# Two heads of four turned in 32x32 squares by VectorE, gathered step by step, with four small moves between engines

## The chip, the cores and the metric

The kernel runs on one core of a Trainium2 chip. The metric is device microseconds of one execution, lower is better; the median of several executions is given. All data are float32. The engines are TensorE (PE in the profile, PEld its weight loads), VectorE (DVE), ScalarE (ACT), GpSimd (POOL) and SyncE (SP), which here only issues DMAs.

## The reference

Two layers run on 8 samples of 512 tokens by 512 features.

The first is a graph attention: features of the tokens and of a condition go through a linear layer; each token attends with 16 heads, in two directions, to the first 20 tokens of its sample; the result goes through a relu and is added to the input. The change doesn't touch it.

The second is a self-attention between two conditioned layer norms:

```python
h = sln(hidden, w)                       # gamma(w) * layernorm(hidden) + beta(w)
q, k, v = split(h @ Wqkv.T + bqkv)       # 16 heads of 32
energy = einsum('bhqd,bhkd->bhqk', q, k)
att = softmax(energy, axis=-1) / D ** 0.5
out = einsum('bhqk,bhkd->bhqd', att, v)
h1 = (out @ Wp.T + bp) + hidden
return sln(h1, w) + h1
```

## The kernel before

The first layer takes the start of the program, to about 397 us of the span. The rest is the second layer, in 128 steps: a step is one batch (sample) b, one group g of four heads and one block c of 128 query tokens, 16 steps to a batch. `at` is the number of the step in its batch. The 112 steps of the first seven batches run in one loop, written out by hand (no scheduler reorders it: each engine runs its instructions in the order of the code); the last batch's 16 steps run in a loop of their own. All of the following is one iteration, step n.

*Scores.* `scores(n + 1)` makes the energies of four heads on TensorE, four heads at a time in four groups of 32 rows, into two pairs of PSUM banks (tile s). `tops` takes the negated maxima of each row on VectorE (one instruction for head 0, one for head 1, one for heads 2 and 3). `exps` takes the exponentials on ScalarE into tiles e, with the sum of each row. Only two pairs of s exist, so the next scores of a pair wait for its exponentials.

*Turning.* For the product with v the exponentials must lie with the keys in the partitions. `turn_probs` does this for a head with four transposes on TensorE into a bank (tile pt), and `keep_probs` copies the bank to turned_et on ScalarE. Heads 0, 1 and 2 go this way (`BY_BLOCK = 3`): heads 0 and 1 at the end of the step before, head 2 behind the scores. Head 3 goes through `turn_blocks`: VectorE transposes its 32x32 squares in place of one another (tile blocks), two steps into one tile; `put_out` writes that tile to DRAM (squares) in every odd step, and in the even step after it `gather` reads it back with four DMAs, one for each block of 32 partitions, so that the squares come to lie where a whole transpose would have put them (tile gathered). Both go through SP's queue, with the loads of tokens (`fetch`), the gates (`load_gate`) and the stores of results.

*Product with v.* In odd steps `weigh_two` multiplies both steps' turned exponentials by v, the four heads side by side in four groups of 32 columns of pao; heads 0 to 2 are of the steps just done, head 3 is two steps older. Every four steps `outputs` copies pao to ao on ScalarE and `divide` applies the sums on GpSimd.

*Projections.* Each step has two slots for products of other batches, listed in `JOBS`: the q, k and v products of the next batch and the output projection of the one before. They are made by a scheme of seven products of halves instead of eight (`product`, `output_product`): each fills a bank and VectorE adds it to where it belongs; the first of the seven (n = 1) is only copied, or gets its bias. The scheme's sums of operands are on GpSimd. These products, the turned heads, the turned tokens (`turn`, tile pz) and the sums' factors (`spread`, tile pr) share three PSUM banks in rotation (`bank`), so a product waits until the bank three allocations earlier has been emptied.

*Norms.* `statistics` (VectorE, with one power on GpSimd) and `norm` make the first norm's z for the batch after next in steps 13 to 15; `finish` does the second norm of the batch before in steps 7 to 12: statistics and norm on VectorE, then three sums on GpSimd and a store. In the code a step's statistics stand behind its two products and the exchange of squares.

Of the kernel before, what the change touches and what calls it, by code (L numbers as in the profile page):

```python
# [19 lines left out]
P = 128  # L20
# [24 lines left out]
def graph_then_self_attention(ctx: ExitStack, tc: tile.TileContext, x, x_t, near, near_t, labels, w_self_t, wq, wk_t,  # L45
# [679 lines left out]
    bp = ctx.enter_context(tc.tile_pool(name="bp", bufs=2, reuse_waits="tile"))  # L725
# [57 lines left out]

    def product(b, i, n):

        a = {1: lambda: a_(i, 0, 0), 2: lambda: a_(i, 0, 1), 3: lambda: SUMS[i, 3], 4: lambda: a_(i, 1, 1),
             5: lambda: SUMS[i, 0], 6: lambda: SUMS[i, 1], 7: lambda: SUMS[i, 2]}[n]()
        t = {1: lambda: quarter(HT[b], 0, 0), 2: lambda: quarter(HT[b], 1, 0), 3: lambda: quarter(HT[b], 1, 1), 4: lambda: SUMS["t", 3],
             5: lambda: SUMS["t", 0], 6: lambda: SUMS["t", 1], 7: lambda: SUMS["t", 2]}[n]()
        out = bank(f"pst_{b}_{i}_{n}").rearrange("p (m n) -> p m n", m=2)  # L790
        fixed, moving = (t, a) if i == 2 else (a, t)
        for m in range(2):
            for k in range(2):
                nc.tensor.matmul(out[:, m, :], fixed[:, k, m * P:(m + 1) * P], moving[:, k, :], start=(k == 0), stop=(k == 1))  # L794
# [12 lines left out]
        if n == 1 and i < 2:  # L807
            bias_2 = col["b_q" if i == 0 else "b_k"][:, 2:4].unsqueeze(2).to_broadcast([P, 2, M])
            nc.vector.tensor_tensor(c_(1, 0), out, bias_2, ALU.add)
        elif n == 1:  # L810
            nc.vector.tensor_copy(c_(1, 0), out)
        for dst, src in {2: [((0, 0), (1, 0))], 6: [((1, 0), (1, 0))], 5: [((1, 1), (1, 0))], 3: [((0, 1), (1, 1))],
                         4: [((1, 0), (1, 0))], 7: [((1, 1), (1, 1)), ((1, 0), (1, 0))]}.get(n, ()):
            if i < 2 and n in (2, 3):
                for j in range(2):
                    nc.vector.scalar_tensor_tensor(c_(*dst)[:, j, :], out[:, j, :], b_less[:, i, j:j + 1], c_(*src)[:, j, :], ALU.add, ALU.add)
            else:
                nc.vector.tensor_tensor(c_(*dst), out, c_(*src), ALU.add)
# [9 lines left out]
    def output_product(b, n):  # L828
# [135 lines left out]
    def spread(m):  # L964
# [7 lines left out]
    BY_BLOCK = 3  # L972
    turned_et = tp.tile([P, 2, BY_BLOCK, C, P], F32, name="turned_et")
    gathered = xp.tile([P, C, F], F32, tag="x", name="gathered").rearrange(
        "p k f -> p (k f)").rearrange(
        "p (i r k c q) -> p i r k c q", i=2, r=4, k=C, c=2)
# [12 lines left out]
    def keep_probs(n, j, copy):  # L989
        pt = PT[n, j]  # L990
        if j < BY_BLOCK:
            et = turned_et[:, n % 2, j]
        else:
            et = bp.tile([P, C, P], F32, tag="blocks", name=f"et_{n}_{j}")
# [3 lines left out]
    def turn_blocks(n):  # L998

        if n % 2 == 0:  # L1000
            BLOCKS[n // 2] = bp.tile([P, 4, C, 2, DH], F32, tag="blocks", name=f"blocks_{n // 2}")
        nc.vector.transpose(BLOCKS[n // 2][:, :, :, n % 2, :].rearrange("p s k q -> p k s q"),  # L1002
                            E[n][BY_BLOCK].rearrange("p (k s q) -> p k s q", k=C, s=4))

    def put_out(m):

        OUT[m] = dram.tile([P, 4, C * 2 * DH], F32, tag="squares", bufs=3, name=f"squares_{m}")
        nc.sync.dma_start(OUT[m], BLOCKS[m].rearrange("p s k c q -> p s (k c q)"))

    def gather(m):  # L1010

        by_chunk = OUT[m].rearrange("(r p) s e -> s p r e", r=4)
        for s in range(4):
            nc.sync.dma_start(gathered[DH * s:DH * (s + 1), m % 2].rearrange("p r k c q -> p r (k c q)"), by_chunk[s])
# [14 lines left out]
    def weigh_two(m):  # L1029

        for k in range(C):
            for j in range(4):
# [5 lines left out]
                moving = turned_et[:, :, j, k, :] if j < BY_BLOCK else gathered[:, m % 2 ^ 1, :, k].rearrange("p r c q -> p c r q")  # L1038
# [46 lines left out]
    from_v3 = made(v, 3) + made(q, 1, 2) + made(v, 7, 4) + made(q, 6, 5)  # L1085
    JOBS = {0: own + made(v, 1, 2, 6, 5) + from_v3 + made(k, 1, 2, 6) + [None] + made(q, 3) + end}
# [5 lines left out]
    JOBS[B - 2][14:] = (made(v, 3) + made(q, 1, 2) + [None] + made(q, 6, 5) + made(k, 1) + [None] + made(k, 2, 6) + made(q, 3)  # L1092
# [25 lines left out]
    def job(b, slot):  # L1118
# [11 lines left out]
        elif kind == "late":  # L1130
            product(b, *of)
        elif kind == "output":
# [4 lines left out]
    with tc.manual_schedule():  # L1137
# [16 lines left out]
        for j in range(BY_BLOCK - 1):  # L1154
            turn_probs(0, j)

        for n, (b, g, c) in enumerate(steps[:ALONE]):
            at = n % 16
            scores(n + 1)
            turn_probs(n, BY_BLOCK - 1)  # L1160
            for j in range(BY_BLOCK - 1):
# [5 lines left out]
            keep_probs(n, BY_BLOCK - 1, nc.scalar.copy)  # L1167
            if n > 4 and n % C == 2:
                divide(n // C - 1)
            turn_blocks(n)  # L1170
            if n % C == C - 1:
# [10 lines left out]
            if n == 5:  # L1182
                values_bias()
# [9 lines left out]
            if n % 2:  # L1193
                weigh_two(n // 2)
            if n % 2 == 0 and n > 0:
                gather(n // 2 - 1)
            elif n % 2:
                put_out(n // 2)
            if b == 0:
                weight_sums((v, q, k, 3)[at // 4], at % 4)  # L1200
            finish_parts(b, "statistics")
            if b + 2 < B:
                for i in {13: (0, 1), 14: (2, 3)}.get(at, ()):
                    norm_stats(b + 2, i)
# [3 lines left out]
            finish_parts(b, "sums")  # L1208
            if at != 4:
                add_gathered()  # L1210
            exps(n + 1, range(4))
            if n + 1 < ALONE:
                for j in range(BY_BLOCK - 1):
# [18 lines left out]
        for n in range(ALONE, len(steps)):  # L1232
# [27 lines left out]
            if at == 0:  # L1260
                spread(n // C - 1)
                outputs(n - 1, slice(0, DH * BY_BLOCK))
                gather(n // 2 - 1)
# [80 lines left out]
```

## Time and profile before

| what | value |
|---|---|
| runs | 1316.15, 1312.71, 1314.56 us; median 1314.56 |
| profiled execution | 1310.33 us; its span 1308.5 us |
| granted TensorE clock | 0.999 |
| TensorE busy | 1283.5 us, 98% of the span |
| VectorE, ScalarE, GpSimd busy | 960.2 (73%), 740.6 (57%), 627.9 us (48%) |
| a steady batch (16 steps) | 111.78 us; TensorE 111.30, VectorE 82.70, ScalarE 78.72, GpSimd 50.77 busy |
| DMA queue of SP | 142.30 MB, 32.8% of 16 engines' time |

A row of the profile names the line of the kernel, the engine, the operation, the tiles written and read, and the number of instructions; then busy time, mean duration in ns, and idle time of the engine just before them with what ended it. The chain that ended last follows the program back from its last instruction, at each piece to what released it. SPq is SyncE issuing DMAs.

### The profile page before, as it was taken

The numbers are of one execution on the slowest core, as the hardware profiler recorded it, in microseconds if no ns is written. First come the engines' busy times: TensorE is split into PE (matmuls) and PEld (weight loads), VectorE is DVE, ScalarE is ACT, GpSimd is POOL, SyncE is SP. The second block draws the span as 40 slices with busy tenths as digits, with TensorE's granted clock in tenths as the row PEclk, the third lists the DMA queues.
The fourth block names the chain that finished last, engine by engine and source line by source line (L and its number), as shares of the span: only waits on it lengthen the run. The fifth ranks groups of instructions, "written<-read, shape, count | busy, mean of one in ns | idle before, by whom it ended". The sixth has DMA issues, their size and how long they took to land.

```text
span 1308.5 us, 24813 instructions
## 1 busy us (share of the span) xinstructions
PE 1283.5 (98%) x9227; PEld 917.2 (70%) x9227; DVE 960.2 (73%) x1675; ACT 740.6 (57%) x1790; POOL 627.9 (48%) x537
## 2 busy tenths in 40 slices
PE   9999999999999999999999999999999999999997
PEld 6567887777764577677777767667776776766775
DVE  4479897888745568768858766876876777676887
ACT  2333233323224666767776676676667677676664
POOL 0067765677650112337235623733643363373776
PEclk9999999999999999999999999999999999999999
DMA  9533552253221132413422342432243243233010
GB/s 343 181 110 104 191 195 104 84 178 111 92 76 46 65 98 65 146 65 121 134 85 81 130 129 65 151 124 82 90 133 118 72 139 133 78 111 101 9 42 34
DMA packets 90486, 144.42 MB, mean 110 GB/s; under 512 B 14272, under 2 KB 47488, under 8 KB 90368
## 3 DMA queue, kind: packets, MB, share of 16 engines
q1 hardware_dynamic: 89936, 142.30, 32.8%
q8 instruction: 74, 1.21, 0.4%
q10 hardware_dynamic: 432, 0.55, 0.1%
q14 instruction: 44, 0.36, 0.1%
HBM read 95.97 MB, written 46.85 MB: 109 GB/s over the span
## 4 chain that ended last, share of the span: by engine, by line
PE 90%; DVE 7%; ACT 1%; POOL 1%; issue 1%; DMA 0%; POOLq 0%; DVEq 0%; ACTq 0%
PE pst L794 19%; PE pt L987 15%; PE s L929 12%; PE pao L1039 8%; PE pss L533 8%; PE psp L837 6%; PE psf_p L360 4%; PE psf L313 2%; PE pqk L139 2%; PE po L577 2%; PE ppj L865 2%; PE pw L502 1%; PE ptw L565 1%; PE pq L483 1%; PE pao L1026 1%; PE pv L139 1%
## 5 line engine op out<-in xcount | busy, mean ns | idle before, releaser
L934 DVE TENSOR_REDUCE top<-s 128x1 f32<-128x512 f32 (+1 forms) x369 | 306.5, 884 | 96.3 <-PE s L929 96.1
L948 ACT ACTIVATE e<-s,top 128x512 f32<-128x512 f32 x512 | 345.6, 692 | 44.8 <-DVE top L934 43.5
L996 ACT COPY turned_et<-pt 128x512 f32<-128x512 f32 x369 | 205.8, 592 | 200.3 <-PE pt L987 200.2
L987 PEld LDWEIGHTS pt<-ident,e 128*128 128x128 f32 x1600 | 174.8, 140 | 132.1 <-issue 60.0
L987 PE MATMUL pt<-ident,e 128*128 128x128 f32 x1600 | 230.7, 280 | 4.6 <-ACT e L948 3.2
L929 PE MATMUL s<-k_pair,q_pair 32*128 32x512 f32 x992 | 159.4, 640 | 0.0
L533 PE MATMUL pss<-kq,sf 128*128 128x320 f32 x512 | 142.9, 432 | 0.0
L1064 POOL TENSOR_TENSOR ao_pair<-ao_pair,factor 128x512 f32<-128x512 f32 x28 | 36.8, 1313 | 188.3 <-ACT ao_pair L1059 188.3
L533 PEld LDWEIGHTS pss<-kq,sf 128*128 128x128 f32 x512 | 94.9, 190 | 36.1 <-ACT kq L490 0.3
L1039 PE MATMUL pao<-turned_et,v 128*32 128x256 f32 x1344 | 107.9, 382 | 0.0
L948 ACT ACTIVATION_READ_ACCUMULATOR e<-s,top 128x1 f32 x512 | 107.3, 209 | 0.0
L1039 PE MATMUL pao<-gathered,v 128*32 128x256 f32 x448 | 107.2, 382 | 0.0
L1002 DVE STREAM_TRANSPOSE blocks<-e 128x512 f32<-128x512 f32 x112 | 79.0, 706 | 23.2 <-ACT e L948 22.9
L1039 PEld LDWEIGHTS pao<-turned_et,v 128*32 128x32 f32 x1344 | 49.9, 109 | 48.3 <-issue 13.5
L539 POOL TENSOR_TENSOR t<-t,mask 128x640 f32<-128x640 f32 x32 | 49.5, 1546 | 65.3 <-DVE t L537 65.3
L554 ACT ACTIVATE t<-t 128x640 f32<-128x640 f32 x32 | 23.6, 738 | 93.3 <-POOL t L551 93.3
L929 PEld LDWEIGHTS s<-k_pair,q_pair 32*128 32x128 f32 x992 | 48.1, 182 | 29.6 <-issue 18.5
L559 POOL TENSOR_TENSOR t<-t,den 128x640 f32<-128x640 f32 x32 | 40.7, 1272 | 56.3 <-DVE den L558 55.7
L551 POOL TENSOR_TENSOR t<-t,top 128x640 f32<-128x640 f32 x32 | 47.3, 1480 | 39.0 <-DVE top L550 39.0
L961 POOL TENSOR_SCALAR wide<-dens 128x512 f32<-128x512 f32 x28 | 42.1, 1503 | 48.8 <-ACT turned_et L996 34.7
L97 POOL TENSOR_TENSOR mv<-mv,minus_half 128x1 f32<-128x1 f32 x32 | 19.6, 611 | 92.7 <-DVE mv L96 92.7
L956 POOL TENSOR_SCALAR e<-e,den 128x512 f32<-128x512 f32 x63 | 46.3, 735 | 28.0 <-DVE den L953 18.7
(290 smaller groups left out, 2572.8 us busy)
## 6 DMA issues: line engine op xcount, KB each, us to landing
squares<-blocks SPq DMA_DIRECT2D x56, 512.0 KB
gathered<-squares SPq DMA_DIRECT2D x224, 128.0 KB
x<-in_x SPq DMA_DIRECT2D x8, 1024.0 KB
mid<-x SPq DMA_DIRECT2D x32, 256.0 KB
xq<-mid SPq DMA_DIRECT2D x8, 1024.0 KB
out<-o SPq DMA_DIRECT2D x31, 256.0 KB
vt<-in_x_t SPq DMA_DIRECT2D x7, 1024.0 KB
xn<-mid SPq DMA_DIRECT2D x7, 1024.0 KB
```

Source lines behind the costliest of these rows:

```text
L360: nc.tensor.matmul(o[:, m, :], a[:, k, m * P:(m + 1) * P], t[:, k, :], start=(k == 0), stop=(k == 1))
L533: nc.tensor.matmul(o, SF[b][:, k, cut], KQ[b][:, k, on], start=(k == 0), stop=(k == C - 1))
L539: nc.gpsimd.tensor_tensor(t, t, MASK[b][:, c, None].to_broadcast([P, H, D2]), ALU.mult)
L794: nc.tensor.matmul(out[:, m, :], fixed[:, k, m * P:(m + 1) * P], moving[:, k, :], start=(k == 0), stop=(k == 1))
L837: nc.tensor.matmul(out[:, m, :], t[:, k, m * P:(m + 1) * P], a[:, k, :], start=(k == 0), stop=(k == 1))
L929: nc.tensor.matmul(S[n][j // 2][:, j % 2, :], Q[b, g][on, c * P:(c + 1) * P], K[b, g][on, :], start=True, stop=True)
L934: nc.vector.tensor_reduce(top, S[n][pair][:, j:j + len(heads)], AX.X, ALU.max, negate=True)
L948: nc.scalar.activation(e, S[n][j // 2][:, j % 2, :], AF.Exp, bias=TOP[n, j], accum_out=den)
L987: nc.tensor.transpose(pt[:, k * P:(k + 1) * P], E[n][j][:, k * P:(k + 1) * P], ident)
L996: copy(et, pt.rearrange("p (k n) -> p k n", k=C))
L1002: nc.vector.transpose(BLOCKS[n // 2][:, :, :, n % 2, :].rearrange("p s k q -> p k s q"), E[n][BY_BLOCK].rearrange("p (k s q) -> p k s q", ...
L1039: nc.tensor.matmul(pao[DH * j:DH * (j + 1), c * P:(c + 2) * P], V[b][:, k, DH * h:DH * (h + 1)], moving, start=(k == 0), stop=(k == C - 1))
```

## The change

- `BY_BLOCK` is 2: head 2 joins head 3 on VectorE's way, so `turn_blocks` has two transposes per step, into one tile per step. `put_out` and `gather` run in every step, right behind `turn_blocks`; a step's squares are gathered in the next one. The pool of blocks has one buffer instead of two, and there are two tiles gathered instead of two halves of one.
- The transposes of both remaining heads stand at the end of the step before, ahead of `weigh_two` in odd steps; none stands behind the scores.
- The first of each seven products is emptied by ScalarE instead of VectorE. These copies are kept in `LATER` and run between the exponentials of heads 1 and 2.
- z is made by GpSimd instead of VectorE, from batch 2 on.
- A step's statistics move ahead of its products, right behind the maxima.
- In `JOBS` some products change places, v's and q's within a step above all; the product for the values' bias becomes a job.

```diff
-        nc.vector.tensor_scalar(Z[b][:, c, :], (src or XN[b])[:, c, :], mv[:, 0:1], mv[:, 1:2], ALU.subtract, ALU.mult)
+        engine = nc.gpsimd if src is None and b > 1 else nc.vector
+        engine.tensor_scalar(Z[b][:, c, :], (src or XN[b])[:, c, :], mv[:, 0:1], mv[:, 1:2], ALU.subtract, ALU.mult)
...
-    bp = ctx.enter_context(tc.tile_pool(name="bp", bufs=2, reuse_waits="tile"))
+    bp = ctx.enter_context(tc.tile_pool(name="bp", bufs=1, reuse_waits="tile"))
...
-            bias_2 = col["b_q" if i == 0 else "b_k"][:, 2:4].unsqueeze(2).to_broadcast([P, 2, M])
-            nc.vector.tensor_tensor(c_(1, 0), out, bias_2, ALU.add)
+            for j in range(2):
+                LATER.append(lambda j=j, dst=c_(1, 0): nc.scalar.activation(
+                    dst[:, j, :], out[:, j, :], AF.Identity, bias=col["b_q" if i == 0 else "b_k"][:, 2 + j:3 + j]))
         elif n == 1:
-            nc.vector.tensor_copy(c_(1, 0), out)
+            LATER.append(lambda dst=c_(1, 0): nc.scalar.copy(dst, out))
...
-                nc.vector.tensor_copy(Y[b], out)
+                LATER.append(lambda dst=Y[b]: nc.scalar.copy(dst, out))
...
-    BY_BLOCK = 3
+    BY_BLOCK = 2
...
     def turn_blocks(n):
-        if n % 2 == 0:
-            BLOCKS[n // 2] = bp.tile([P, 4, C, 2, DH], F32, tag="blocks", name=f"blocks_{n // 2}")
-        nc.vector.transpose(BLOCKS[n // 2][:, :, :, n % 2, :].rearrange("p s k q -> p k s q"),
-                            E[n][BY_BLOCK].rearrange("p (k s q) -> p k s q", k=C, s=4))
+        BLOCKS[n] = bp.tile([P, 4, C, 2, DH], F32, tag="blocks", name=f"blocks_{n}")
+        for h in range(2):
+            nc.vector.transpose(BLOCKS[n][:, :, :, h, :].rearrange("p s k q -> p k s q"),
+                                E[n][BY_BLOCK + h].rearrange("p (k s q) -> p k s q", k=C, s=4))
...
-    from_v3 = made(v, 3) + made(q, 1, 2) + made(v, 7, 4) + made(q, 6, 5)
...
-                   + from_v3 + made(k, 1, 2, 6) + made(q, 3) + [None] + end)
+                   + made(q, 1) + made(v, 3) + made(q, 2) + made(v, 7, 4) + made(q, 6) + made(k, 1) + made(q, 5)
+                   + made(k, 2, 6) + [None] + made(q, 3) + end)
...
             scores(n + 1)
-            turn_probs(n, BY_BLOCK - 1)
-            for j in range(BY_BLOCK - 1):
+            for j in range(BY_BLOCK):
                 keep_probs(n, j, nc.scalar.copy)
...
             turn_blocks(n)
+            put_out(n)
+            if n > 0:
+                gather(n - 1)
...
+            finish_parts(b, "statistics")
+            if b + 2 < B:
+                for i in {13: (0, 1), 14: (2, 3)}.get(at, ()):
+                    norm_stats(b + 2, i)
             if 0 < at <= C:
                 turn(b + 1, at - 1)
...
             job(b, 2 * at)
             finish_parts(b, "norm")
             job(b, 2 * at + 1)
-            if n % 2:
-                weigh_two(n // 2)
-            if n % 2 == 0 and n > 0:
-                gather(n // 2 - 1)
-            elif n % 2:
-                put_out(n // 2)
...
-            finish_parts(b, "statistics")
...
+            exps(n + 1, (0, 1))
+            for after in LATER:
+                after()
+            LATER.clear()
             if at != 4:
                 add_gathered()
-            exps(n + 1, range(4))
+            exps(n + 1, (2, 3))
             if n + 1 < ALONE:
-                for j in range(BY_BLOCK - 1):
+                for j in range(BY_BLOCK):
                     turn_probs(n + 1, j)
...
+            if n % 2:
+                weigh_two(n // 2)
```

More of the change, by code (lines that the diff above doesn't have):

```diff
@@ L782, in graph_then_self_attention @@
     b_less = w1.tile([P, 2, 2], F32, name="b_less")
+    LATER = []
     def product(b, i, n):
@@ L970, in spread @@
         nc.scalar.copy(factor, pr)
-    BY_BLOCK = 3
+    BY_BLOCK = 2
     turned_et = tp.tile([P, 2, BY_BLOCK, C, P], F32, name="turned_et")
-    gathered = xp.tile([P, C, F], F32, tag="x", name="gathered").rearrange(
-        "p k f -> p (k f)").rearrange(
-        "p (i r k c q) -> p i r k c q", i=2, r=4, k=C, c=2)
+    gathered = [xp.tile([P, C, F], F32, tag="x", name="gathered_0").rearrange("p k f -> p (k f)"),
+                tp.tile([P, C * F], F32, name="gathered_1")]
+    gathered = [t.rearrange("p (c r k h q) -> p c r k h q", c=2, r=4, k=C, h=2) for t in gathered]
     pao = ps_a.tile([P, 512], F32, tag="pao", name="pao")
@@ L993, in keep_probs @@
         else:
-            et = bp.tile([P, C, P], F32, tag="blocks", name=f"et_{n}_{j}")
+            et = gathered[0][:, n % 2].rearrange("p r k h q -> p (r k h q)").rearrange("p (j k n) -> p j k n", j=2, k=C)[:, j - BY_BLOCK]
         ET[n, j] = et
@@ L998, in turn_blocks, with put_out, gather @@
     def turn_blocks(n):
-        if n % 2 == 0:
-            BLOCKS[n // 2] = bp.tile([P, 4, C, 2, DH], F32, tag="blocks", name=f"blocks_{n // 2}")
-        nc.vector.transpose(BLOCKS[n // 2][:, :, :, n % 2, :].rearrange("p s k q -> p k s q"),
-                            E[n][BY_BLOCK].rearrange("p (k s q) -> p k s q", k=C, s=4))
[L1005 to L1012, printed above, removed]
+        BLOCKS[n] = bp.tile([P, 4, C, 2, DH], F32, tag="blocks", name=f"blocks_{n}")
+        for h in range(2):
+            nc.vector.transpose(BLOCKS[n][:, :, :, h, :].rearrange("p s k q -> p k s q"),
+                                E[n][BY_BLOCK + h].rearrange("p (k s q) -> p k s q", k=C, s=4))
+    def put_out(n):
+        OUT[n] = dram.tile([P, 4, C * 2 * DH], F32, tag="squares", bufs=3, name=f"squares_{n}")
+        nc.sync.dma_start(OUT[n], BLOCKS[n].rearrange("p s k h q -> p s (k h q)"))
+    def gather(n):
+        by_chunk = OUT[n].rearrange("(r p) s e -> s p r e", r=4)
         for s in range(4):
-            nc.sync.dma_start(gathered[DH * s:DH * (s + 1), m % 2].rearrange("p r k c q -> p r (k c q)"), by_chunk[s])
+            nc.sync.dma_start(gathered[n // 2 % 2][DH * s:DH * (s + 1), n % 2].rearrange("p r k h q -> p r (k h q)"), by_chunk[s])
     def weigh(n):
@@ L1037, in weigh_two @@
                 h = 4 * g + j
-                moving = turned_et[:, :, j, k, :] if j < BY_BLOCK else gathered[:, m % 2 ^ 1, :, k].rearrange("p r c q -> p c r q")
+                moving = turned_et[:, :, j, k, :] if j < BY_BLOCK else gathered[m % 2 ^ 1][:, :, :, k, j - BY_BLOCK, :]
                 nc.tensor.matmul(pao[DH * j:DH * (j + 1), c * P:(c + 2) * P], V[b][:, k, DH * h:DH * (h + 1)],
@@ L1084, in graph_then_self_attention @@
     end = made(k, 5, 3) + first + fifth + made(q, 4, 7)
-    from_v3 = made(v, 3) + made(q, 1, 2) + made(v, 7, 4) + made(q, 6, 5)
-    JOBS = {0: own + made(v, 1, 2, 6, 5) + from_v3 + made(k, 1, 2, 6) + [None] + made(q, 3) + end}
+    JOBS = {0: own + made(v, 1) + [("values_bias",)] + made(v, 2, 6) + made(q, 1) + made(v, 5, 3) + made(q, 2) + made(v, 7, 4)
+            + made(k, 1) + made(q, 6, 5) + made(k, 2, 6) + made(q, 3) + end}
     for b in range(1, B - 1):
@@ L1089, in graph_then_self_attention @@
                    + made(v, 2, 6) + [("output", 1, 7)] + made(v, 5) + [("output", 1, 4)]
-                   + from_v3 + made(k, 1, 2, 6) + made(q, 3) + [None] + end)
-    JOBS[B - 2][14:] = (made(v, 3) + made(q, 1, 2) + [None] + made(q, 6, 5) + made(k, 1) + [None] + made(k, 2, 6) + made(q, 3)
+                   + made(q, 1) + made(v, 3) + made(q, 2) + made(v, 7, 4) + made(q, 6) + made(k, 1) + made(q, 5)
+                   + made(k, 2, 6) + [None] + made(q, 3) + end)
+    JOBS[B - 2][14:] = (made(q, 1) + made(v, 3) + made(q, 2) + [None] + made(q, 6, 5) + made(k, 1) + [None] + made(k, 2, 6) + made(q, 3)
                         + made(k, 5, 3) + made(q, 4) + [None] + made(q, 7) + made(k, 4) + made(k, 7))
@@ L1131, in job @@
             product(b, *of)
+        elif kind == "values_bias":
+            values_bias()
         elif kind == "output":
@@ L1166, in graph_then_self_attention @@
                 outputs(n - 3, slice(DH * BY_BLOCK, P))
-            keep_probs(n, BY_BLOCK - 1, nc.scalar.copy)
-            if n > 4 and n % C == 2:
                 divide(n // C - 1)
             turn_blocks(n)
+            put_out(n)
+            if n > 0:
+                gather(n - 1)
             if n % C == C - 1:
@@ L1181, in graph_then_self_attention @@
                 spread(n // C - 1)
-            if n == 5:
-                values_bias()
             if at in OUTPUT_SUMS_AT:
@@ L1192, in graph_then_self_attention @@
             job(b, 2 * at + 1)
-            if n % 2:
-                weigh_two(n // 2)
-            if n % 2 == 0 and n > 0:
-                gather(n // 2 - 1)
-            elif n % 2:
-                put_out(n // 2)
             if b == 0:
                 weight_sums((v, q, k, 3)[at // 4], at % 4)
-            finish_parts(b, "statistics")
             if b + 2 < B:
-                for i in {13: (0, 1), 14: (2, 3)}.get(at, ()):
-                    norm_stats(b + 2, i)
                 for i in {14: (0, 1), 15: (2, 3)}.get(at, ()):
@@ L1208, in graph_then_self_attention @@
             finish_parts(b, "sums")
+            exps(n + 1, (0, 1))
+            for after in LATER:
+                after()
+            LATER.clear()
             if at != 4:
                 add_gathered()
-            exps(n + 1, range(4))
+            exps(n + 1, (2, 3))
             if n + 1 < ALONE:
-                for j in range(BY_BLOCK - 1):
+                for j in range(BY_BLOCK):
                     turn_probs(n + 1, j)
@@ L1262, in graph_then_self_attention @@
                 outputs(n - 1, slice(0, DH * BY_BLOCK))
-                gather(n // 2 - 1)
+                gather(n - 1)
             job(b, 2 * at)
```

## The prediction

> **What bounds the kernel now.** I read the page's engine sums first, then the chain that ended last inside one steady batch, then busy time by stretch of that batch, and last the rows of VectorE and of the DMA queue. The sums:
>
> ```profile
> PE 1283.5 (98%) x9227; PEld 917.2 (70%) x9227; DVE 960.2 (73%) x1675; ACT 740.6 (57%) x1790; POOL 627.9 (48%) x537
> ```
>
> TensorE is busy 98% of the span, but a share says nothing of order, so here is the chain (start, length, piece) over steps 7 and 8 of batch 3, from one group of scores to past the next:
>
> ```profile
> 801.47 1.07 PE s L929 x8
> 802.54 0.59 PE pt L987 x4
> 803.13 3.46 PE pst L794 x16
> 806.58 1.86 PE pao L1039 x32
> 808.45 1.02 PE pt L987 x8
> 809.47 1.07 PE s L929 x8
> 810.54 0.59 PE pt L987 x4
> 811.13 0.44 PE pr L968 x4
> 811.57 3.46 PE pst L794 x16
> 815.02 0.87 PE pt L987 x8
> ```
>
> Nothing but TensorE stands in it. An odd step is 1.07 + 0.59 + 3.46 + 1.86 + 1.02 = 8.00 us, an even one without the last product of probabilities 5.99, and a head's four transposes are on the path. They cost 0.59 us behind the scores, but four such transposes behind a full-array piece (pr) only 0.44: 0.15 is the switch from tiles of 32 rows to the whole array, and it is paid again (1.02 against 0.87) behind pao. Now the same batch in three stretches: steps 0 to 7, 8 to 11, 12 to 15 (start and end, length, then busy time of PE, PEld, DVE, ACT and POOL, clock, DMA share, GB/s):
>
> ```profile
> 753.59:809.40 55.81, 55.33 (x417) 39.04 (x416) 36.73 (x55) 41.13 (x101) 16.52 (x14) 1.00 0.36 114
> 809.40:837.82 28.42, 28.42 (x214) 20.55 (x213) 23.99 (x41) 19.23 (x48) 18.82 (x17) 1.00 0.28 88
> 837.82:865.37 27.55, 27.55 (x205) 19.28 (x204) 21.98 (x41) 18.36 (x46) 15.43 (x15) 1.00 0.37 122
> ```
>
> VectorE (DVE) is busy 36.73 of 55.81, but 23.99 of 28.42 and 21.98 of 27.55: it is in the second half of a batch that it has little to spare. The batch is 111.8 us; batches 1 to 5 agree within 1.3 us, and 112 steps run this way (397 to 1198 us). What precedes and the last batch's row of projections keep their work.
>
> **What the change does to TensorE.** Per step it removes one head's four transposes, 0.44 us (the switch of 0.15 falls to the product that now follows the scores). If the block's whole 0.59 went, it would be 0.15 more. In odd steps the transposes move ahead of pao and scores follow pao instead: the switch may vanish (0.15 gained) or be paid by the scores; no row shows pao followed by s, and I take it as paid, as the other two switches are. So 16 x 0.44 = 7.04 us per batch, from below; 16 x 0.59 = 9.44 from above. The order of the products is otherwise only swapped within a step, and the bias of the values is one product, once.
>
> **VectorE.** It gains a second stream transpose per step, and loses four evacuations of first products and four normalizations per batch:
>
> ```profile
> L1002 DVE STREAM_TRANSPOSE blocks<-e 128x512 f32<-128x512 f32 x112 | 79.0, 706 | 23.2 <-ACT e L948 22.9
> 810.58 2.42 DVE L934 TENSOR_REDUCE top<-s 128x1 f32<-128x512 f32 x3 [1.62 <-PE s L929]
> 813.33 0.88 DVE L816 SCALAR_TENSOR_TENSOR q_pair<-pst,b_less,q_pair 128x256 f32<-128x256 f32 x2 [0.34 <-PE pst L794]
> 814.12 0.54 DVE L879 TENSOR_SCALAR o<-xq,mv_h 128x512 f32<-128x512 f32 x1
> 815.06 1.29 DVE L818 TENSOR_TENSOR v<-pst,v 128x512 f32<-128x512 f32 x2 [0.40 <-PE pst L794]
> ```
>
> Plus 16 x 0.706 = 11.3, less 4 x 0.69 (L809, L811, L846) and 4 x 0.54 (L112): 82.7 becomes 89.1 in a batch that TensorE would run in 104.8. By stretch: 36.73 + 5.6 - 1.4 = 41.0 of 52.3; 23.99 + 2.8 - 0.7 = 26.1 of 26.7; 21.98 + 2.8 - 0.7 - 2.2 = 21.9 of 25.8. In steps 8 to 11 there is 2% left, and these are waits that can't all be filled. So I walk it, with t = 0 where the scores end.
>
> In an ordinary even step the maxima run 0.05 to 2.47, the first exponential starts at 0.8, and the last ends at about 4.1 (0.69 each). The next scores for heads 2 and 3 need that; TensorE comes to them at 3.61 + 0.87 + 0.5 = 5.0. So VectorE may start the maxima some 0.85 late at no cost. An odd step is 1.86 longer and stands more.
>
> Step 8: VectorE does maxima to 2.47, statistics (0.68 + 0.18 + 0.15 with gaps 1.08, now ahead of the sums) to 3.55, 0.88, 0.54, 1.29, then both transposes 1.4: free at 7.7, while TensorE's next scores end after 0.59 + 3.46 + 0.87 + 1.07 = 5.99. Maxima of step 9 start 1.7 late and end at 4.1; statistics to 5.2; only then the sum that empties v4's bank, 5.9. The banks rotate by three, and that bank is the next but two: the second transposed head waits for it, and TensorE was there at 4.05. Stall 1.9. Step 13: the light step before leaves transposes late by 0.85; maxima to 3.3, two statistics 2.1, sum to 6.1 against 4.05: 2.05. Step 15: step 14's two statistics and the double sum leave it 1.75 late; q4's sum ends at 5.1 against 4.05: 1.05. Step 11: 0.15. Together 5.15 us of 7.04 given back. Steps 0, 1, 2 and 12, with one product each, are held by this chain already (5.20, 7.45, 5.45 and 4.82 with 0.74 left to step 13: 23.7, where an even one has 4.70 of TensorE work); with one copy fewer on ScalarE ahead of the exponentials I get 4.6, 6.4, 5.3 and 4.5, or 20.8, which is 1.1 better than the 4 x 0.44 counted above. Net 7.04 + 1.1 - 5.15 = 3.0 per batch.
>
> **ScalarE and GpSimd.** ScalarE loses 16 copies (592 ns each by L996) and gains four first products per batch: 0.36 for 128x240 (L488) makes 0.8 for the two halves, 0.6 for whole copies. They stand between the second and third exponential, but the third waits for its maximum until 2.6 while the second ends at 2.15, so they delay the last to 4.5 or so: below 5.0, nothing. If that cover is gone, 0.4 x 4 = 1.6 per batch. Deferring them holds a bank until 3.1; TensorE needs it at 4.05: nothing. GpSimd takes 4 z at 0.69 (L956, 63 such) per batch, busy 50.8 of 111.8, and z is wanted a step later: nothing, at most the step's 1.27 of a sum ahead of it.
>
> The z rows of VectorE run 0.526 to 0.545 us, but L879, the same form, has single ones up to 1.283 beside GpSimd work. The Trainium skill ("SBUF — State Buffer", section "SBUF: two separate sides") says that such a VectorE instruction and a GpSimd one exclude each other for a whole instruction; by that rule, which speaks against moving z, each z could return up to its own 0.69 to VectorE, 2.8 per batch against 2.2 saved, and the sum would be 3 us per batch of stall more at worst, not 0. Rows favour the saving: 31 instructions of L879 have a median of 0.537.
>
> The skill also advises ("VectorE: DVE Perf Modes", section "The three transpose paths") TensorE for whole 128x128 transposes, since VectorE turns only 32x32 squares. By that advice the change should lose; by the rows VectorE's 0.706 is longer than TensorE's 0.44 and needs a round trip besides, and wins only as far as VectorE has room.
>
> **The queue and the round trip.** Squares go out every step instead of every second, so per step 1 + 4 issues on SP (0.34 + 1.74 us), and 77 GB/s beside the 109 of now: share of the DMA engines 0.34 to some 0.58. Gathers land more than a step before use. Only one buffer of squares stays: the next transposes wait until the write is through, and behind them on VectorE stand the maxima. In the trace the gather waits for that write:
>
> ```profile
> 801.97 0.34 SPq L1008 DMA_DIRECT2D squares<-blocks  x1
> 804.64 2.83 SPq L1014 DMA_DIRECT2D gathered<-squares  x4
> SPq L1014 <- DMA squares<-blocks: 52.1, 18, 4.7
> ```
>
> 2.7 us here, 2.9 on average of 18 waits, up to 4.8 from issue (787.99 to 792.75). Between the end of one step's transposes and the start of the next I count 3.9 to 4.5 us in the tight places, so it costs 0 to 0.9 there, within the 0.85 that is free. I take 0. A 1 MB fetch ahead of it on the queue, or a store that waits for GpSimd, could make single ones longer.
>
> **Sum.** 7 x 3.0 = 21. Batch 0 has no rows to finish and no stall in step 9, 1.9 more: 23. The profiled execution took 1310.33 (span 1308.5), 4.2 below the median of 1314.56; a saving carries over, so 1314.56 - 23 = 1291.5. With the switch behind pao gone as well, 8 x 0.15 x 7 = 8.4 less.
>
> **Rivals.** (1) VectorE keeps up everywhere and nothing is given back: 7 x (7.04 + 1.1) = 57, so 1257.5; with the 8.4, 1249. For it: 89.1 of 104.8. Against: the 98% of steps 8 to 11. Chance 0.18. (2) Slower, by the single buffer of squares: with more traffic the write takes L; in the 8 steps per batch that follow a short one the transposes wait L - 4.1, of which 0.85 is free. From L = 5.33 this eats the 3.0; at L = 6, 8 x 1.05 = 8.4, net 5.4 per batch, 1352. For it: 4.8 was seen, and traffic grows by 70%. Against: the mean is 2.9, and the write stands ahead of the step's gathers. Chance 0.18. (3) The stalls of the walk are twice as long, since a fetch of the next tokens lands late for the statistics, which now come some 2 us sooner in step 13, or since waits on VectorE don't overlap: 10.3 given back, 2.2 per batch worse, 1330. Chance 0.14. (4) The forecast, 0.50, own range 1275 to 1308.
>
> **Range and chances.** (1) reaches from 1249 to the forecast as stalls shrink, and a third of it, 0.06, lies below 1262. Above 1332 lie 0.10 of (2), whose price begins at nothing and grows with L, and 0.04 of (3). That leaves 0.2 out. A difference of 0.3% (4 us) is about what a measurement of this kernel can tell from none. Faster: 0.46 of (4), all of (1), 0.02 of (3): 0.66. Same: 0.03 of (4), 0.03 of (3), 0.01 of (2): 0.07. Slower: 0.17 of (2), 0.09 of (3), 0.01 of (4): 0.27.
>
> **What would show it.** Right: pt behind the scores gone from the chain; steps 5 and 6 at 7.4 to 7.6 and at 5.55 us; VectorE at 88 to 90 per batch; TensorE waiting for VectorE's sums ahead of the second transposed head in steps 9, 13 and 15; steady batch near 108.5. Wrong: VectorE's transposes waiting for the squares' write for microseconds per step, or batches at 104 without any wait of TensorE.

## The result, and the profile after

The changed kernel takes 1319.87 us (median of 6 runs, 1317.54 to 1322.65); the kernel before, beside it, 1314.03 us (6 runs, 1311.55 to 1316.15). The ratio is 1.0047 with a 95% interval of 1.0026 to 1.0067. So the change is slower by 5.8 us where 23 us less were forecast. The profiled execution took 1322.56 us, its span is 1320.8 us and its mean granted clock 0.987.

The engine sums of the changed kernel and its queue for data (packets, MB, share):

```profile
PE 1262.6 (96%) x8779; PEld 881.6 (67%) x8779; DVE 995.7 (75%) x1736; ACT 699.1 (53%) x1719; POOL 678.7 (51%) x561
q1 hardware_dynamic: 130256, 201.04, 50.1%
```

TensorE runs 448 transposes fewer and is busy 20.9 us less (a group of scores that waits half-way and products at a lower clock count as busy: in step 13 below, 1.88 and 3.57 us instead of 1.07 and 1.86), and yet the span is 12.3 us longer: TensorE now waits. Counted from the scores of step 0 to those of the next batch, batches 1 to 5 took 111.9, 114.8, 116.2, 116.3 and 113.8 us, where the forecast was near 109; before, batch 1 took 113.0 and batches 2 to 5 took 111.8 each. That they now differ among themselves is a first sign of something that is not fixed by the order of the code. Batch 3 as a whole, then its steps 9 and 13 (start and end, length, busy time of PE, PEld, DVE, ACT and POOL, clock, DMA share, GB/s):

```profile
747.91:864.12 116.21, 109.37 (x769) 73.65 (x768) 87.09 (x146) 72.82 (x183) 59.13 (x48) 0.97 0.60 177
815.77:825.31 9.54, 7.87 (x65) 5.04 (x64) 9.17 (x16) 3.95 (x11) 6.74 (x7) 1.00 0.51 139
843.56:858.07 14.51, 10.55 (x65) 6.16 (x65) 8.34 (x16) 4.90 (x14) 2.80 (x4) 0.80 0.63 195
```

Step 9 is VectorE's: busy 9.17 of 9.54. Step 13 is nobody's: 14.51 us, with VectorE busy 8.34 of it, and the clock of TensorE is 0.80 there. The chain that ended last shows both, step 9 first:

```profile
818.84 2.31 DVE top L938 x3
...
821.15 0.61 DVE st_h L93
...
822.07 0.69 DVE v L822
...
822.89 0.63 PE pt L991 x4
823.52 1.86 PE pao L1043 x32
```

This is the stall that the forecast described: maxima, then statistics, then the sum that empties v4's bank, and only then the second transposed head. Step 13 has another chain:

```profile
842.47 8.14 DMA xn<-mid
...
850.63 0.70 DVE st L93
...
852.73 0.61 DVE k_pair L822
...
853.48 1.09 PE pt L991 x4
854.57 3.57 PE pao L1043 x32
858.14 1.53 PE s L933 x8
```

Three instructions of the same stretch, with the idle time of the engine before one and what ended it in brackets:

```profile
844.92 2.38 DVE L938 TENSOR_REDUCE top<-s 128x1 f32<-128x512 f32 x3
850.63 0.69 DVE L93 BATCH_NORM_STATS2 st<-xn 128x6 f32<-128x512 f32 x1 [3.32 <-DMA xn<-mid]
853.48 1.09 PE L991 MATMUL pt<-ident,e 128*128 128x128 f32 x4 [3.96 <-DVE k_pair L822]
```

The fetch of the next tokens lands 8.14 us after its issue. VectorE is through with the maxima at 847.30 and stands at the statistics until the landing, 3.32 us; the sum for TensorE's bank stands behind them, and TensorE, which has waited 3.96 us, then goes on at a lower clock: pao takes 3.57 us against 1.86 in step 9. Over the whole program VectorE waited 13.9 us for this fetch (first line; the third is of SyncE's queue, from 633 to 1094 us):

```profile
DVE st L93 <- DMA xn<-mid: 13.9, 5, 3.8
DVE blocks L1006 <- DMA squares<-blocks: 13.2, 5, 3.2
SPq L102 <- POOL z L113: 10.1, 4, 2.6
```

(total us, times, longest.) The other two lines are one more chain, through steps 0 to 2: the fetch of step 0 waits on SyncE's queue for GpSimd's z, whose buffer it takes; the squares' write is issued behind that 1 MB fetch; and VectorE's next transposes wait for the write, since there is one buffer:

```profile
760.65 1.39 DVE blocks L1006 x2
...
762.05 6.86 DMA squares<-blocks
...
769.01 1.30 DVE blocks L1006 x2
```

### The profile page after: what moved, and what is told of

Its sections match the earlier page's. It is cut to its first block, busy times and chain, and to the rows that moved or that the text cites. A ratio compares the mean times of both kernels' runs of the same rounds, so it can differ in the third digit from the quotient of the medians.

```text
span 1320.8 us, 24381 instructions
## 1 busy us (share of the span) xinstructions
PE 1262.6 (96%) x8779; PEld 881.6 (67%) x8779; DVE 995.7 (75%) x1736; ACT 699.1 (53%) x1719; POOL 678.7 (51%) x561
## 4 chain that ended last, share of the span: by engine, by line
PE 69%; DVE 17%; DMA 7%; ACT 3%; issue 2%; SPq 1%; POOL 1%; POOLq 0%; DVEq 0%; ACTq 0%
PE pst L797 11%; PE s L933 9%; PE pss L534 8%; PE pt L991 7%; PE pao L1043 7%; PE psp L841 5%; DVE top L938 4%; PE psf_p L361 4%; DMA xn<-mid 3%; DMA squares<-blocks 3%; ACT e L952 3%; DVE blocks L1006 3%; PE pqk L140 2%; PE psf L314 2%; PE po L578 2%; PE ppj L869 2%
## 5 line engine op out<-in xcount | busy, mean ns | idle before, releaser
L1000 ACT COPY turned_et<-pt 128x512 f32<-128x512 f32 x241 | 131.0, 596 | 149.5 <-PE pao L1043 143.7
L991 PE MATMUL pt<-ident,e 128*128 128x128 f32 x1152 | 164.8, 279 | 36.9 <-DVE k_pair L822 18.8
L991 PEld LDWEIGHTS pt<-ident,e 128*128 128x128 f32 x1152 | 130.7, 142 | 78.6 <-ACT e L952 41.3
L1006 DVE STREAM_TRANSPOSE blocks<-e 128x512 f32<-128x512 f32 x224 | 147.3, 692 | 36.8 <-ACT e L952 18.8
L933 PE MATMUL s<-k_pair,q_pair 32*128 32x512 f32 x992 | 168.0, 645 | 1.0 <-ACT e L952 0.4
L1043 PE MATMUL pao<-turned_et,v 128*32 128x256 f32 x896 | 112.7, 396 | 0.0
L1043 PE MATMUL pao<-gathered,v 128*32 128x256 f32 x896 | 112.7, 396 | 0.0
```

The source lines that it names most:

```text
L933: nc.tensor.matmul(S[n][j // 2][:, j % 2, :], Q[b, g][on, c * P:(c + 1) * P], K[b, g][on, :], start=True, stop=True)
L991: nc.tensor.transpose(pt[:, k * P:(k + 1) * P], E[n][j][:, k * P:(k + 1) * P], ident)
L1000: copy(et, pt.rearrange("p (k n) -> p k n", k=C))
L1006: nc.vector.transpose(BLOCKS[n][:, :, :, h, :].rearrange("p s k q -> p k s q"), E[n][BY_BLOCK + h].rearrange("p (k s q) -> p k s q", k=C, ...
L1043: nc.tensor.matmul(pao[DH * j:DH * (j + 1), c * P:(c + 2) * P], V[b][:, k, DH * h:DH * (h + 1)], moving, start=(k == 0), stop=(k == C - 1))
```

## The experiments

Times are medians. Ratios are against the kernel before, run beside each on the same chip (medians 1313.12 to 1313.76). "Batch" is the mean of batches 1 to 5 of the profiled execution, a time of a step that of batch 3 where nothing else is said. Before it is 112.0 us, after 114.6.

**Both statistics back behind the products.** From the changed kernel:

```diff
-            finish_parts(b, "statistics")
-            if b + 2 < B:
-                for i in {13: (0, 1), 14: (2, 3)}.get(at, ()):
-                    norm_stats(b + 2, i)
             if 0 < at <= C:
                 turn(b + 1, at - 1)
...
+            finish_parts(b, "statistics")
+            if b + 2 < B:
+                for i in {13: (0, 1), 14: (2, 3)}.get(at, ()):
+                    norm_stats(b + 2, i)
```

> The change with both kinds of statistics (of the rows to finish and of the fetched tokens) put back behind a step's products, as in the kernel before. Theory H (the statistics stand ahead of the sum that empties a bank, and the second transposed head waits for that bank): step 9 falls from 9.54 us to about 7.6, step 13 from 12.3 to 15.0 us to about 7.6, steps 11 and 15 from 8.0 to about 7.6; six batches: about 30 + 10 + 4 us, so near 1276 us. Rival V (VectorE is simply full, the order doesn't matter): the waits move to other steps, 1310 us or more. Rival D (DMA traffic makes writes and fetches late, whatever waits for them): step 13 stays above 10 us, 1300 to 1315 us.

Measured: 1299.81 us (1299.47 to 1302.04), ratio 0.9901 [0.9880, 0.9922]. Batch 110.8. Steps 13 and 15 of batch 3:

```profile
835.00:843.20 8.20, 8.20 (x66) 5.43 (x65) 6.49 (x12) 4.90 (x14) 2.27 (x3) 1.00 0.83 270
849.09:858.20 9.11, 8.62 (x66) 5.33 (x65) 8.81 (x18) 4.45 (x13) 7.27 (x6) 1.00 0.47 132
```

So this one edit of the change, which removes no work and adds none, costs 20 us; without it the rest of the change is 1.0% faster than before. Step 13 falls from 14.51 to 8.20, TensorE is busy in all of it, and the clock is 1.00. Step 9 falls from 9.54 to 8.23. Step 15 gets longer, 9.11 against 8.02 (8.5 to 9.4 over batches 1 to 5): two statistics stand late in step 14 there. The size was missed by 24 us; what is left lies in step 15 and in steps 0 to 3, which this edit doesn't mend: the squares' write took 7.02 us in this run too. The fetch is late here as well, up to 9.0 us after its issue, and costs less: VectorE waits 2.7 us for it in the whole program instead of 13.9.

**Only the fetched tokens' statistics back.** The `norm_stats` lines alone are moved as above.

> The change with only the statistics of the fetched tokens (steps 13 and 14) put back behind the products; those of the rows to finish stay ahead. Theory H: step 13 comes down to about 7.6 us, step 9 stays at 9.5; about 30 us gained of the 44 of a_stats_back, near 1290 us. Rival V: 1310 us or more. Rival D: step 13 above 10 us, 1300 to 1315 us.

Measured: 1308.46 us (1305.01 to 1314.04), 0.9968 [0.9952, 0.9985], some 18 us above the size that was expected. Step 13 of batch 3:

```profile
841.72:849.91 8.19, 8.19 (x65) 5.43 (x64) 6.73 (x12) 4.89 (x14) 0.79 (x2) 1.00 0.85 266
```

The two stalls come apart: step 13 goes with the statistics of fetched tokens (11.4 us of time), step 9 with those of the second norm, and stays at 9.54 until these go back too (8.7 us more).

**Statistics ahead in the kernel before.** The same move, made alone on the kernel before.

> The kernel before with only the statistics moved ahead of the products, nothing else. Theory H: before, the product with v stands ahead of the transposes in odd steps and covers the sum that comes later (1.86 us), and VectorE has 0.7 us less in each step, so nothing or little: 1312 to 1319 us. Rival S (the place of the statistics alone costs, with any number of turned heads): steps 9 and 13 lengthen by 1 us or more, 1322 us or more.

Measured: 1317.02 us (1315.10 to 1320.63), 1.0025 [1.0011, 1.0039], within the first expectation. Batch 112.6; step 14 grows from 5.99 to 6.91, step 9 by 0.2, step 13 not at all. So the move by itself costs 3 to 4 us where VectorE has room, and 20 us in the changed kernel, where VectorE has one transpose more per step, the queue carries more, and the product with v no longer stands ahead of the transposes on TensorE: the price is not the edit's own.

**The product with v back ahead of the transposes,** nothing else changed:

```diff
             exps(n + 1, (2, 3))
+            if n % 2:
+                weigh_two(n // 2)
             if n + 1 < ALONE:
...
-            if n % 2:
-                weigh_two(n // 2)
```

> The change itself with one thing undone: in odd steps the product with v stands ahead of the transposes again, as in the kernel before. Theory H (the second transposed head waits for a bank that VectorE empties late; 1.86 us of product would cover that): step 9 falls from 9.54 us to about 7.7, step 13 by 1.9, steps 11 and 15 to 7.6: 3.5 us or more per batch, 1290 to 1300 us instead of 1320. Rival (the scores then stand right behind the transposes and wait for the exponentials of heads 2 and 3, which the product covered): 1315 us or more.

Measured: 1294.11 us (1292.63 to 1307.17), 0.9869 [0.9816, 0.9922], within the first expectation. Steps 9 and 13 of batch 3:

```profile
804.69:812.37 7.68, 7.68 (x66) 5.05 (x65) 7.61 (x14) 4.35 (x12) 4.87 (x6) 1.00 0.43 134
831.03:843.23 12.20, 9.00 (x66) 5.63 (x65) 7.31 (x15) 5.48 (x15) 2.53 (x4) 0.94 0.65 193
```

Step 9's stall is gone although the statistics are still ahead: the 1.86 us of pao now lie where TensorE waited for v4's sum. Step 13 is 8.35 where the fetch is in time and up to 12.20 where it isn't (VectorE still waits 9.7 us for it in all). So it takes both edits to lose: with either of them undone (the statistics behind the products again, or the product with v ahead again) the kernel is 13 to 19 us faster than before. Step 11 grows, from 8.00 to 8.35. In steps 5 and 7, which have no stall, the same edit costs 0.15 us (7.61 against 7.46): the switch of tiles behind pao is paid ahead of pt and not ahead of s.

**z back on VectorE.** `nc.vector.tensor_scalar` for every z, as before the change; statistics stay ahead.

> The change with z back on VectorE. GpSimd's z took 2.08 us each in the profile, and the fetch in step 0 waited up to 2.6 us for it. Theory H: a small matter; the fetch of step 0 and the squares' write behind it come some 2 us sooner (steps 1 to 3 gain 1 us together), VectorE has 1.1 us more in steps 14 and 15 each: 1315 to 1322 us. Rival Z (slow z on GpSimd is what costs, through the queue or through VectorE's port): step 13 and steps 0 to 3 recover, 1300 us or less.

Measured: 1341.65 us (1336.16 to 1345.43), 1.0211 [1.0180, 1.0242]: both expectations missed. Step 15 of batch 3, and the chain in it:

```profile
875.40:887.10 11.70, 9.70 (x69) 5.95 (x68) 11.10 (x18) 4.00 (x12) 4.68 (x4) 0.85 0.33 91
```

```profile
876.63 2.34 DVE z L112 x2
878.96 1.21 DVE blocks L1005 x2
```

VectorE is busy 11.10 of 11.70 us in step 15, z takes up to 1.49 us instead of 0.53, and the two stand ahead of the transposes. Step 15 takes 10.3 to 12.0 in batches 1 to 5, and step 13 still waits for its fetch (8.9 to 14.7). So in this order of the code the move of z away from VectorE is worth 21.8 us, with all that its longer time on GpSimd costs.

**z on ScalarE, with the statistics back.** GpSimd makes only the 128x1 bias, and ScalarE applies it behind the last exponential:

```diff
+            nc.gpsimd.tensor_scalar(less, mv[:, 0:1], mv[:, 1:2], -1.0, ALU.mult, ALU.mult)
+            Z_LATER.append(lambda: nc.scalar.activation(z, x, AF.Identity, bias=less, scale=mv[:, 1:2]))
```

> a_stats_back with z made by ScalarE (scale and bias per row; the bias, minus mean times scale, by one small GpSimd instruction), behind the exponentials of heads 2 and 3 in steps 14 and 15. In a_stats_back's chain four z of 2.07 us each on GpSimd hold the power of the next statistics, the factors (wide) and the fetch of step 0. Theory P (this chain is what is left of steps 15 and 0): step 15 falls from 9.4 to about 8, step 0 from 5.4 to 4.7, some 2 us per batch: 1284 to 1290 us. Rival S (ScalarE delays the copies of turned heads as much): 1297 us or more.

Measured: 1297.09 us (1295.17 to 1300.55), 0.9876 [0.9852, 0.9899], 2.7 us below the version with both statistics back (the two intervals overlap) and just in the rival's range. Step 0 falls from 5.42 to 4.64. That is not the fetch: in the next run but one the fetch is gone from step 0, z is on GpSimd, and step 0 stays at 5.43. It is the factors (wide), which stand behind z on GpSimd, with TensorE's spread (pr) waiting for them; the chain of that run (fetch in quarters) has

```profile
743.67 2.06 POOL z L118
...
748.32 1.51 POOL wide L970
...
749.87 0.66 PE pr L977 x4
```

With z on ScalarE wide ends 2.5 us before step 0 begins, and pr doesn't wait. Step 15 grows to 10.22, since ScalarE now waits for z's bias (total us, times, longest, from 633 to 1090 us):

```profile
ACT z L118 <- POOL less L116: 14.5, 5, 3.4
```

GpSimd only stands last in that wait: its product takes 0.26 us, and in batch 3 it had itself been idle for 3.91 us. What is late are VectorE's statistics of step 14, behind that step's sums again.

**First products back on VectorE, with the statistics back.**

```diff
-            LATER.append(lambda dst=c_(1, 0): nc.scalar.copy(dst, out))
+            nc.vector.tensor_copy(c_(1, 0), out)
```

and the like for the other two places.

> a_stats_back with the first products (v, q, k and the output's) emptied by VectorE again, at once, as before the change. Theory H (VectorE's order and load hold TensorE in the second half of a batch; ScalarE has room): steps 7, 10 and 14 lengthen by some 0.7 us or push their neighbours, 1 to 2 us per batch: 1305 to 1315 us against 1300. Rival L (the deferred copies between the exponentials cost as much as they save): 1298 to 1302 us.

Measured: 1301.53 us (1300.32 to 1302.16), 0.9905 [0.9885, 0.9925], against 1299.81 with them on ScalarE; the two ranges overlap, as the rival had it. Step 3 gets shorter by 0.48 and step 11 longer by 0.58. The move to ScalarE gives on one side what it takes on the other.

**Step 0's fetch in quarters, with the statistics back.** The 1 MB for the second norm goes out in four parts, in steps 3, 5, 7 and 9:

```diff
-            if at == 0 and 0 < b:
-                fetch(b)
+            if at in (3, 5, 7, 9) and 0 < b:
+                fetch_quarter(b, (at - 3) // 2)
```

> a_stats_back with the 1 MB fetch of step 0 (tokens for the residual, first used in step 11) split into four of 256 KB in steps 3, 5, 7 and 9. Theory Q (the squares' write of step 1 stands behind that fetch on the queue, 7.0 us instead of 3, and with one buffer the transposes and maxima wait): steps 1 and 2 fall from 7.1 and 6.1 to 6.5 and 5.3, about 1.5 us per batch: 1288 to 1292 us. Rival (those steps are held by the chain of maxima and exponentials alone): 1298 us or more.

Measured: 1291.76 us (1290.30 to 1294.23), 0.9834 [0.9815, 0.9854], as the expectation that gave 1288 to 1292 had it. Step 2 of batch 3, with the fetch in one piece (first line) and in quarters:

```profile
760.41:766.53 6.12, 4.96 (x32) 2.89 (x28) 3.61 (x5) 4.51 (x10) 2.49 (x2) 1.00 0.78 235
760.32:765.31 4.99, 4.53 (x33) 3.00 (x29) 2.42 (x3) 4.63 (x10) 2.50 (x2) 1.00 0.82 245
```

The squares' write no longer stands behind the fetch, and step 2 falls to 4.99 in all batches. VectorE's waits for the squares' write, 15.7 us in the version with the fetch in one piece, don't appear any more. That is the chain through steps 0 to 2, shown by its removal: 8 us. Steps 1 and 3 stay at 7.12 and 9.06, so they weren't held by it.

**Both of the last two together** (z on ScalarE, fetch in quarters).

> Both of the two: z on ScalarE and the fetch in quarters, on top of a_stats_back. Theories P and Q together: 4 us per batch, 1274 to 1280 us, a version ahead of both kernels. If both wait on the same thing (the fetch that stands behind z), no more than the better one alone, about 1286 us.

Measured: 1293.34 us (1290.30 to 1298.87), 0.9849 [0.9819, 0.9880]: no better than the quarters alone, neither expectation met. Step 0's 0.8 us go into step 15, at 9.4 to 12.2.

**The second pair of statistics ahead in step 14, the first behind the products in step 13,** with the fetch in quarters.

> i_fetch_apart (statistics behind the products, fetch in quarters) with the second pair of statistics of the fetched tokens ahead of the products in step 14 again; the first pair stays behind in step 13. Theory P (z of step 15, and with it GpSimd's queue, waits for the statistics of step 14): step 15 falls from 9.4 to about 8.0, step 13 stays at 8.2: 1.4 us per batch, 1280 to 1284 us against 1292. Rival: step 14 pays it back, 1290 us or more.

Measured: 1286.86 us (1285.94 to 1287.99), 0.9792 [0.9768, 0.9817], between the two expectations. In batches 1 to 3 step 15 is 8.23, where it was 9.39 with the quarters alone, and step 13 stays at 8.2; in batch 4, where the fetch took 9.73 us to land, step 14 is 7.63 and step 15 11.42, with a lower clock. Step 0 falls too, from 5.43 to 4.64: z and the factors come 1.2 us sooner on GpSimd. So placing statistics ahead pays in step 14, where the data have mostly landed, and not in step 13.

**The same with the product with v ahead of the transposes.**

> k_split_stats with the product with v ahead of the transposes in odd steps as well. Theory H: the 0.5 to 0.8 us that are left over 7.46 in each of steps 9, 11, 13 and 15 go: 1266 to 1276 us. Rival (scores wait for exponentials): at or above k_split_stats.

Measured: 1283.90 us (1281.91 to 1284.89), 0.9767 [0.9742, 0.9793]: the best version found, 30 us below the kernel before and 36 below the changed one, but 8 us above the expected range. Batch 108.0; batch 3, and one piece of the chain in it:

```profile
742.80:851.80 109.00, 107.47 (x770) 72.32 (x769) 87.61 (x146) 72.82 (x183) 58.94 (x49) 1.00 0.63 189
```

```profile
826.99 9.24 DMA xn<-mid
```

Step 9 is 7.61 us with TensorE busy for all and VectorE for 7.50 of it. The two heads on VectorE's way are all still there, so what lost the time was not they but what was moved with them. The fetch of the next tokens still takes 9.24 us to land, and two of five batches still have a step 14 of 7.0 and 6.8 us instead of 5.6. The chain that ended last runs on VectorE from 801 to 822 us, steps 9 to 11, without a break longer than 0.7, and from there through the issue of a squares' write to this fetch.

**VectorE's transpose made twice in the kernel before,** nothing moved; the second one writes the same values again.

> The kernel before with its one VectorE transpose made twice per step into the same place: 0.7 us more of VectorE per step, nothing taken from TensorE, no more transfers. Theory H (room of VectorE alone is not the matter while the bank's sums are covered by the product with v): VectorE 94 of 112 us per batch, 1314 to 1324 us. Rival V (VectorE full): 1330 us or more.

Measured: 1326.52 us (1321.86 to 1326.99), 1.0095 [1.0066, 1.0124], between the two expectations. Batch 3 takes 113.3 us:

```profile
759.10:872.40 113.30, 112.04 (x835) 78.81 (x834) 92.44 (x153) 79.00 (x193) 50.77 (x44) 1.00 0.32 108
```

Of 16 steps only two grow: step 0 by 0.93 and step 15 by 0.57. So VectorE busy for 9.7 us more per batch (92.44 against 82.70) costs 1.5 us. This is the order of before, with the product with v as cover and TensorE's work whole; in the best version, with TensorE's work cut, VectorE is busy 87.61 of 109.0. VectorE's total, then, is not what the change lost by; it is where the work stands.

## Why the prediction was wrong

The sign was wrong: rival (3), "a fetch of the next tokens lands late for the statistics", with 1330 and a chance of 0.14, is what happened in the main. By steps (us per batch from step 0 to step 15, mean of batches 1 to 5; forecast worked out from the prediction's terms):

| steps | forecast | measured | difference |
|---|---|---|---|
| 0 to 2 | 4.6 + 6.4 + 5.3 = 16.3 | 4.70 + 7.12 + 5.77 = 17.6 | +1.3 |
| 3 | 8.73 - 0.44 = 8.29 | 9.08 | +0.8 |
| 9 | 8.00 - 0.44 + 1.9 = 9.46 | 9.54 | +0.1 |
| 11 | 8.00 - 0.44 + 0.15 = 7.71 | 8.00 | +0.3 |
| 12 and 13 | 4.5 + 8.00 - 0.44 + 2.05 = 14.1 | 4.65 + 13.10 = 17.75 | +3.6 |
| 14 | 5.99 - 0.44 = 5.55 | 5.85 | +0.3 |
| 15 | 8.00 - 0.44 + 1.05 = 8.61 | 8.02 | -0.6 |
| 4 to 8, 10 | 38.75 | 38.6 | -0.1 |
| batch | 108.8 | 114.5 | +5.7 |

**TensorE's part held.** Steps 5 and 6 are 7.46 and 5.60 us, within 0.05 of the forecast 7.4 to 7.6 and 5.55. Two small terms in it were off and partly cancel: the switch behind pao, taken as paid, is not paid ahead of scores (0.15, shown by putting pao back); the product that follows the scores takes 3.65 us instead of 3.46, so 0.19 of the switch falls there and not 0.15.

**VectorE's amount nearly held** (87.09 in batch 3, of 88 to 90 forecast and 89.1 added up: the second transpose was priced like the first, 0.706, and the pair takes some 1.3 us), and so did the walk where it needs VectorE alone. Step 9 is 9.54, and its chain is the one forecast. The exception is step 15, forecast with 1.05 of stall and measured with half of that; when the statistics go back behind the products it does lengthen, to 8.5 to 9.4.

**The step that failed: the landing of the fetch in step 13.** The term "maxima to 3.3, two statistics 2.1, sum to 6.1 against 4.05: 2.05" took the data as there. By the prediction's own trace there was no room for that: in batch 3 the walk has the maxima of step 13 end at 843.73 + 3.3 = 847.0, 5.85 us after the fetch's issue at 841.18, and before, the last of a fetch's 16 landings came 5.3 to 6.2 us after its issue. After, the maxima of batch 3 ended 4.83 us after it; the last landing came at 7.1 us in two batches and at 8.1, 8.3, 9.2 and 9.8 in the other four, while the median one moved only from between 4.9 and 5.2 to between 5.3 and 5.8. TensorE's wait there, 2.05 in the sum, was 1.75 to 4.46 us. The prediction had the mechanism (rival 3), but with a chance of 0.14 and no price of its own, beside a queue that it took to carry 70% more in the loop (177 GB/s against 109 in batch 3). Rival 3 was priced as twice the stalls; to the wait itself came, in three of the batches, a lower clock in the rest of the step, which the walk had no term for. That this is the cause of step 13's length is shown: with these statistics alone moved back, step 13 is 8.2 in every batch and 11.4 us are gone. The product with v, which no longer covers the wait, is the other half: with it put back, step 13 is 9.5 on the mean, with the statistics still ahead.

**The second: z and the squares' write at steps 0 to 2.** z on GpSimd was taken at 0.69 us, from L956, and takes 2.08:

```profile
L113 POOL TENSOR_SCALAR z<-xn,mv 128x512 f32<-128x512 f32 x24 | 49.7, 2078 | 0.6
```

L956 has the same shape, but multiplies in place by one factor per row and one constant, where z subtracts and multiplies with two values per row; no run tells which of these differences makes the factor of three. "Nothing" for z's move was therefore wrong at its end: the fetch of step 0 waits for the buffer that z reads, and where z comes later still (both statistics back), the factors behind it on GpSimd make step 0 longer by 0.8 us. And "I take 0" for the squares' write went by the mean of its waits before, 2.9 us; behind a 1 MB fetch the write took 6.86. The prediction's own sentence, "a 1 MB fetch ahead of it on the queue ... could make single ones longer", put no number to this although it happens once per batch at a known place; it measured 8 us (fetch in quarters). Rival (2), the single buffer, is thus right at this one place and wrong elsewhere: the wait came five times in the whole program, 2.6 us each, not in 8 steps of every batch. A second buffer wasn't tried.

**Steps 1 and 3** were forecast too short for another reason: the 6.4 of step 1 supposed that the exponentials of the light step before it would be ready 1.05 sooner. It went from 7.45 to 7.12 only, and is 7.01 in the best version, whose chain still has 1.80 us for the scores in it instead of 1.07: that fits scores that wait half-way for exponentials, as before, where they took 1.81, but no run was made to show it. In step 3 the first product's copy on ScalarE stands between the exponentials and the scores wait for it; with the copies on VectorE step 3 is 0.48 shorter. The prediction named that price ("If that cover is gone, 0.4 x 4 = 1.6 per batch") and one of the four places pays it; since step 11 gains as much, it makes no difference in time.

**The rule on exclusion.** The prediction weighed a page that lets VectorE's z and GpSimd's work exclude each other, and preferred the rows (0.537). With z left on VectorE, its rows in the loop go from 0.53 to 1.49 us (shortest, median, longest ns):

```profile
L112 DVE TENSOR_SCALAR z<-xn,mv x16: 531/778/1491, 640.2 to 997.9; 128x512 f32<-128x512 f32 x16
```

The eight z of 1.01 to 1.49 us all lie beside sums of GpSimd, the eight of 0.53 to 0.54 beside none. Two of the long ones:

```profile
758.87 1.27 POOL L828 TENSOR_TENSOR xq<-y,xq 128x512 f32<-128x512 f32 x1
759.41 2.43 DVE L112 TENSOR_SCALAR z<-xn,mv 128x512 f32<-128x512 f32 x2
760.10 1.45 POOL L116 TENSOR_TENSOR xq<-xq,bp_bc 128x512 f32<-128x512 f32 x1
```

That agrees in direction with what the Trainium skill says ("SBUF — State Buffer", section "SBUF: two separate sides"); no run here takes GpSimd's work away to prove it. In batch 3 of the kernel before no z had begun beside such a sum, so z's rows there (0.526 to 0.545) could not show it. Either way moving z off VectorE was right in this order, by some 3 us per batch where the prediction had counted 2.2 of VectorE's work.

**What stays open:** why a fetch's last landings are late in some batches and not in others. Step 13 varies from batch to batch (10.2 to 15.0) with the same code, and no run separates the number of packets from their order on the queue.

## What to carry to other kernels

Before work is moved ahead on an in-order engine, list what it waits for, a DMA above all, and price the wait with the transfer's late end under the new traffic, not with its landing time of before; whatever stands behind the moved work inherits the wait. A filler that is moved away (here the product with v ahead of the transposes) costs nothing in the sums and a whole stall where it covered one, so look at each pair of edits, not at each edit. An average of busy time says little about slack: VectorE busy for 9.7 us more per batch cost 1.5 us in one order, while statistics moved ahead of the products, with no work added, cost 2.9 us per batch in another.

## What the runs showed of the hardware that was not expected

- GpSimd's `tensor_scalar` on 128x512 float32 took 2.08 us as z (subtract and multiply, two values per row; 2.07 to 2.08 in all 24) and 0.69 us in the median of L956 (two multiplications in place, one value per row and a constant; mean 0.74).
- Of the 16 landings of the next tokens' 1 MB fetch the last came 7.1 to 9.8 us after the issue in the changed kernel, where the median one came at 5.3 to 5.8; before, 5.3 to 6.2 and 4.9 to 5.2.
- In the changed kernel TensorE's granted clock fell to half for 6.83 us in step 13 of batches 2, 3 and 4, where TensorE waited 2.97, 3.96 and 4.46 us; it did not in batch 5, after 3.89 us, nor in batch 1, after 1.80. In batch 3 that makes 0.80 over the step, with the 32 products of pao in 3.57 us instead of 1.86, and the scores behind them in 1.53 instead of 1.07. In the run where the wait was removed the same step had 1.00. So a stall can cost more than its length.
